# Two key tiles in a step for the last, 256-wide block of queries

## The chip, the cores and the metric

The kernel runs on one core of a Trainium2 chip, as one program in one launch. What counts is device time in microseconds (us) from start to end of the program. The core has a matrix engine (PE in the profile, with PEld for the loads of its stationary operand), a vector engine (DVE), an activation engine (ACT), a general engine (POOL) and an engine that issues DMAs (SP). PE writes only to PSUM, which has eight banks of 512 f32 in each of 128 partitions. DVE and ACT read PSUM; POOL works on SBUF.

## The reference

Two layers follow each other, each with a residual and a layer norm. The first is an attention over 3327 nodes by cosine, masked with a sparse adjacency matrix; the change does not touch it. The second is this:

```python
q = (x @ Wq.T).reshape(d, n, h)      # d = 128 groups, n = 3327 nodes, h = 8
k = (x @ Wk.T).reshape(d, n, h)
v = (x @ Wv.T).reshape(d, n, h)
a = jnp.einsum('dnh,dmh->dnm', q, k) * d ** (-0.5)
a = a + adj + adj
a = jax.nn.softmax(a, axis=2)
out = jnp.einsum('dnm,dmh->dnh', a, v)
out = out.reshape(n, h * d) @ Wo.T
```

So there are 128 independent attentions over 3327 x 3327 pairs, with an inner size of only 8, and each pair gets twice its adjacency added ahead of the softmax.

## The kernel before

Nodes are padded to 26 tiles of 128 (T = 26). Queries are cut into nine blocks (NB): eight of three tiles, 384 queries, and a last one of two tiles, 256 queries. The 128 attentions are taken four at a time, so there are 32 groups, and a *unit* is one block with one group: 288 units, the last 32 of them 256 wide. A unit runs 26 *steps*, one for each key tile, so the main loop (line 884) has 7488 steps, 832 of them in the last block. The four attentions of a group are called heads here; each has its own 32 rows of PE, since queries and keys stand in SBUF with 32 partitions for a head (line 228): a high and a low part of each number, times 8, times 2.

Scores stand in PSUM with keys on partitions and queries along the bank. The order of instructions on PE, ACT, DVE and POOL is the order of the code (a manual schedule), each engine taking its own in turn; the order on SP is the framework's. In one step:

- `shifts` (L805) puts minus the maximum of each query's scores into the two banks of `eb`, for two heads; `scores` (L811) adds query times key. ACT takes the exponential of both banks in one instruction (L921, tile `pb`), and POOL multiplies with `eT`, the exponential of twice the adjacency (L922).
- For the other two heads the same happens in two single banks `ea`, but the adjacency is added on PE: `add_adj` (L792) multiplies `aT` with twice the identity, in four column strips a head. ACT takes the exponential of each bank (L946, tile `pa`).
- `weigh` (L822) multiplies the weights `pa` and `pb` with the values and sums over the keys into one bank, `acc`, in four column strips, one a head. It handles the tile of two steps before (LAG = 2). Its operands are f32, and each product is two matmul records. After a unit's last tile, `take` (L833) copies `acc` out.
- `search` finds the maxima of a unit ahead of it: 33 steps ahead (T + AHEAD) it makes products of queries with keys in the other direction (`max_product`, L265), 512 keys at a time, and DVE reduces each to a maximum a query. In the 384-wide blocks a step has one *pair* (two heads, two banks, one reduce of 1024, L280) and one *single* (one head, one bank, a reduce of 512, L301). For the 256-wide units a step has two singles, of heads (2, 3) and (0, 1) in turn (line 237); these take banks from a pool of three (`at_n`, line 901), used in rotation.
- When a unit's maxima are there, `shift_parts` splits them into three bf16 parts, and late in the unit before, `shift_turn` (L778) transposes them on PE; ACT copies them to `cx` (L940).

PSUM is full: two banks `ea`, two `eb`, one `acc`, three for the search. In a step of the last block the search products use the rows of the same two heads as `eb` (line 904).

Of the kernel before, what the change touches and what calls it, by code (L numbers as in the profile page):

```python
# [10 lines left out]
F32 = mybir.dt.float32  # L11
# [8 lines left out]
P = 128  # L20
N = 3327
T = 26
# [23 lines left out]
def gnn_two_layers(  # L46
# [130 lines left out]
    def width(b):  # L177
        return min(QT, T - b * QT) * P
# [49 lines left out]
    def rows(a):  # L228
        return slice(32 * a, 32 * a + KR)
# [82 lines left out]
    def search(step):  # L312
        if step is not None:
            (max_pair if len(step[1]) == 2 else max_single)(*step)
# [403 lines left out]
    with ExitStack() as at:  # L718
# [15 lines left out]
        for vt in vts:  # L734
            nc.gpsimd.memset(vt[:, :, T - 1, :], 0.0)

        def load_adj_tile(b, j):
            n = width(b) // P
            nc.sync.dma_start(  # L739
                aT[:, j, : n * P].rearrange("p (q k) -> p q k", k=P),  # L740
                aT_s[b * QT : b * QT + n, :, j * P : (j + 1) * P].rearrange("q p k -> p q k"),
            )

        def exp_adj_tile(b, j):
            w = width(b)
            nc.scalar.activation(eT[:, j, :w], aT[:, j, :w], AF.Exp, scale=2.0)

        def load_values(u):

            u.vt = vts[u.i % 3]  # L750
            for first, n, rows in ((0, 112, T), (112, P - 113, T), (P - 1, 1, N - (P - 1) * T)):
                nc.sync.dma_start(
                    u.vt.rearrange("p g t r -> p g (t r)")[first : first + n, :, : rows * R9],
                    bass.AP(
                        tensor=v_s.tensor,
                        offset=v_s.offset + (4 * u.g * N + first * T) * R9,
                        ap=[[T * R9, n], [N * R9, 4], [1, rows * R9]],
                    ),
                )
            u.cx = sm.tile([P, QB], BF16, name="cx")  # L760

        def order_keys(u, j):

# [11 lines left out]
        def shift_turn(u, q, dst, start):  # L775
            for h in range(4):
# [8 lines left out]
                    skip_group_check=True,  # L785
                )

        def add_adj(e, u, j):

            for c in range(4):  # L790
                r = slice(32 * c, 32 * c + 32)
                nc.tensor.matmul(  # L792
                    e[r, : u.nq],
                    two[:, r],
                    aT[:, j, : u.nq],
                    start=False,
                    stop=True,
                    tile_position=(0, 32 * c),
                    skip_group_check=True,
                )  # L800

        def shifts(u, es, hs):
            for e, a in zip(es, hs):
                r = slice(32 * a, 32 * a + 3)
                nc.tensor.matmul(  # L805
                    e[:, : u.nq], one[r], u.cx[r, : u.nq], start=True, stop=False, skip_group_check=True
                )

        def scores(u, j, es, hs, stop):
            for e, a in zip(es, hs):  # L810
                nc.tensor.matmul(  # L811
                    e[:, : u.nq],
                    u.kx[rows(a), j * P : (j + 1) * P],
                    u.qx[rows(a), : u.nq],
                    start=False,
                    stop=stop,
                    skip_group_check=True,
                )

        def weigh(u, j, pts):  # L820
            for h in range(4):
                nc.tensor.matmul(  # L822
                    acc[32 * h : 32 * h + H + 1, : u.nq],
                    u.vt[:, h, j],
                    pts[h][:, : u.nq],
                    start=(j == 0),
                    stop=(j == T - 1),
                    tile_position=(0, 32 * h),
                )

        def take(u):
            ot = sm.tile([P, QB], F32, name="ot")
# [12 lines left out]
        with tc.manual_schedule(  # L845
# [31 lines left out]
            e = ps_b.tile([P, 2, 512], F32, name="eb")  # L877
            for q in range(QT):
                shift_turn(us[0], q, e[:, 0, q * P : (q + 1) * P], True)
            nc.scalar.copy(us[0].cx, e[:, 0, :QB])  # L880

            todo = []
            turn = []
            for s in range(NU * T + LAG):
                i, j = divmod(s, T)
                u = us.get(i)
                if u is not None:
                    if j == 2 and i + 2 < NU:
                        load_keys(new_unit(i + 2))
                        load_queries(us[i + 2], own.tile([P, QB], F32R, name="qx"))  # L890
                        load_values(us[i + 2])
                    if j == 12 and i + 4 < G4:
                        gather(i + 4)
                    k = s + T + AHEAD
                    pair, single = max_step(k) or (None, None)

                    behind = pair is not None and len(pair[1]) == 1
                    if behind and Banks.pair is not None:
                        Banks.pair = None
                        search_banks.close()  # L900
                        ps_n = at.enter_context(tc.tile_pool(name="at_n", bufs=3, space=PSUM))
                        Banks.single = lambda: ps_n.tile([P, 512], F32, name="m3")
                    if behind:
                        hs_b = pair[1] + single[1]
                    else:
                        hs_b = (2, 3) if pair is None else tuple(
                            h for h in range(4) if h not in pair[1]
                        )
                    hs_a = tuple(h for h in range(4) if h not in hs_b)

                    e_b = ps_b.tile([P, 2, 512], F32, name="eb")
                    b01 = [e_b[:, x] for x in range(2)]
                    shifts(u, b01, hs_b)
                    if not behind:
                        search(pair)
                    scores(u, j, b01, hs_b, True)
                    if behind:
                        search(pair)
                        search(single)
                    pt_b = pp.tile([P, 2, QB], F32, name="pb")  # L920
                    nc.scalar.activation(pt_b[:, :, : u.nq], e_b[:, :, : u.nq], AF.Exp)  # L921
                    nc.gpsimd.tensor_tensor(  # L922
                        pt_b[:, :, : u.nq],
                        pt_b[:, :, : u.nq],
                        eT[:, j, : u.nq].unsqueeze(1).to_broadcast([P, 2, u.nq]),
                        ALU.mult,
                    )
                    e_a = new_a()
                    shifts(u, e_a, hs_a)
                    if not behind:  # L930
                        search(single)
                    scores(u, j, e_a, hs_a, False)
                    free = e_a[0][:, QB:]
                    x = us.get(i + 1)
                    copies = []
                    q = j - (T - 4)
                    if x is not None and 0 <= q < x.nt:
                        shift_turn(x, q, free, False)
                        copies.append(
                            lambda: nc.scalar.copy(x.cx[:, q * P : (q + 1) * P], free)  # L940
                        )
                    pt_a = pp.tile([P, 2, QB], F32, name="pa")
                    for h, e in enumerate(e_a):
                        add_adj(e, u, j)
                    for h, e in enumerate(e_a):
                        nc.scalar.activation(pt_a[:, h, : u.nq], e[:, : u.nq], AF.Exp)  # L946
                    for f in copies:
                        f()
                    if x is not None and not x.b:
                        order_keys(x, j)  # L950
                        if j == T - 1:
                            keep_keys(x)
                    pts = {}
                    for x in range(2):
                        pts[hs_a[x]], pts[hs_b[x]] = pt_a[:, x], pt_b[:, x]
                    todo.append((u, j, pts))

                    if k % (2 * T) in (T, 2 * T - 1):
                        v = us.get(k // (2 * T) * 2 + (k % (2 * T) > T))
                        if v is not None:  # L960
                            shift_parts(v)
                if s >= LAG:
                    w = todo.pop(0)
                    weigh(*w)
                    if w[1] == T - 1:
                        take(us.pop(w[0].i))

                if turn and turn[0][0] <= s:
                    exp_adj_tile(*turn.pop(0)[1:])
                if u is not None and i + 1 < NU and units[i + 1][0] != u.b:  # L970
                    load_adj_tile(u.b + 1, j)
                    turn.append((s + 5, u.b + 1, j))
# [96 lines left out]
```

## Time and profile before

| what | value |
|---|---|
| median of 3 runs | 15258.02 us (15257.38 to 15259.73) |
| profiled execution, own time | 15255.29 us |
| its span, first to last instruction | 15253.5 us |
| granted PE clock, mean | 0.996 |
| blocks 2 to 8, pb exponentials from 2438 to 13947 us | 1.98 us a step |
| last block, pb exponentials from 13947 to 15153 us | 1.45 us a step |
| PE, DVE, ACT, POOL busy over the span | 99%, 91%, 84%, 90% |

One profiled execution is a list of instructions with start and duration. A timeline line reads: start in us from the span's start, duration in us, engine, line of the kernel, operation, names of what is written and read, shapes, and how many equal instructions in a row are merged; in square brackets, if the engine sat idle before it, for how long and what ended that. The page's first part gives the busy time of each engine, its share of the span and its instructions. A windows line gives, for a stretch, its length, then busy time and number of instructions of each engine, the granted clock, the share of DMA engines in use and GB/s. A matmul's end in the trace is modelled, and matmuls overlap, so a busy PE is not PE at its peak.

### The profile page before, as it was taken

What the parts mean: (1) busy time and instruction counts of PE and PEld (TensorE: products, weight loads), DVE (VectorE), ACT (ScalarE), POOL (GpSimd) and SP (SyncE); (2) the same over time, 40 slices, a digit from 0 to 9 for tenths busy, and PEclk for the clock granted to TensorE, in tenths of its full rate; (3) what the DMA queues carried; (4) which work ended last, traced back from release to release, by engine and by line L of the source; (5) the groups of instructions that cost most, each with busy time, mean ns of one, the idle gap of its engine ahead of it and who ended that gap; (6) DMA issues with size and microseconds to landing.
All of it is one profiled execution on the core that took longest, in us unless ns stands there. A gap on an engine that the chain in (4) does not pass through costs nothing.

```text
span 15253.5 us, 495125 instructions
## 1 busy us (share of the span) xinstructions
PE 15089.0 (99%) x210460; PEld 6723.2 (44%) x210460; DVE 13878.6 (91%) x16267; ACT 12766.2 (84%) x25413; POOL 13770.0 (90%) x8926
## 2 busy tenths in 40 slices
PE   7899999999999999999999999999999999999999
PEld 5534444444444444444444444444444444444556
DVE  8889999999999999999999999999999999998886
ACT  7699998888888888888888888888888888888887
POOL 3489999999999999999999999999999999999888
PEclk9999999999999999999999999999999999999999
DMA  5632221111111111111111111111111111112212
GB/s 198 207 102 102 99 96 60 47 53 47 59 48 48 52 53 54 47 51 49 54 53 47 53 54 50 50 47 60 47 51 49 47 59 47 53 47 63 64 64 84
DMA packets 549346, 996.69 MB, mean 65 GB/s; under 512 B 148249, under 2 KB 492822, under 8 KB 500790
## 3 DMA queue, kind: packets, MB, share of 16 engines
q1 hardware_dynamic: 547126, 965.00, 19.5%
q8 instruction: 1648, 27.00, 0.8%
q14 instruction: 572, 4.69, 0.1%
HBM read 826.75 MB, written 192.54 MB: 67 GB/s over the span
## 4 chain that ended last, share of the span: by engine, by line
PE 95%; DVE 0%; ACT 0%; DMA 0%; SPq 0%; issue 0%; POOL 0%; ACTq 0%; DVEq 0%; POOLq 0%
PE acc L822 30%; PE ea L792 22%; PE m L265 17%; PE eb L805 13%; PE ea L805 9%; PE ea L811 2%; PE ea L778 1%; PE eb L811 1%; PE pp L1017 0%; PE pq L544 0%; PE sc L265 0%; DVE mx L280 0%; SPq L739 0%; DMA orow<-o_s 0%; ACT oT L1014 0%
## 5 line engine op out<-in xcount | busy, mean ns | idle before, releaser
L922 POOL TENSOR_TENSOR pb<-pb,eT 128x768 f32<-128x768 f32 (+1 forms) x7488 | 13176.7, 1767 | 906.8 <-ACT pb L921 466.4
L280 DVE TENSOR_REDUCE mx<-m 128x2 f32<-128x1024 f32 x6369 | 7807.8, 1226 | 959.1 <-PE eb L811 507.6
L921 ACT ACTIVATE pb<-eb 128x768 f32<-128x768 f32 (+1 forms) x7488 | 5903.9, 788 | 2163.9 <-PE eb L811 1810.5
L265 PE MATMUL m<-kn,qx 32*128 32x512 f32 (+1 forms) x23128 | 6553.6, 463 | 0.0
L946 ACT ACTIVATE pa<-ea 128x384 f32<-128x384 f32 (+1 forms) x14976 | 6336.5, 477 | 27.1 <-PE ea L792 10.4
L822 PE MATMUL acc<-pb,vt 128*9 128x384 f32 (+1 forms) x29952 | 5903.1, 474 | 0.1
L822 PE MATMUL acc<-pa,vt 128*9 128x384 f32 (+1 forms) x29952 | 5903.1, 474 | 0.0
L301 DVE TENSOR_REDUCE mx<-m 128x1 f32<-128x512 f32 x7139 | 4798.0, 681 | 134.4 <-PE m L265 49.5
L805 PEld LDWEIGHTS <-one 3*128 3x128 bf16 x29952 | 1412.1, 91 | 5554.0 <-issue 4659.7
L792 PE MATMUL ea<-aT,two 128*32 128x384 bf16 (+1 forms) x59904 | 3714.3, 325 | 0.0
L811 PE MATMUL eb<-qx,kn 32*128 32x384 f32 (+1 forms) x13312 | 3027.0, 451 | 0.0
L811 PE MATMUL ea<-qx,kn 32*128 32x384 f32 (+1 forms) x13312 | 2933.5, 432 | 0.0
L265 PEld LDWEIGHTS m<-kn,qx 32*128 32x128 f32 x23128 | 2723.0, 182 | 206.0 <-DVE mx L301 4.4
L805 PE MATMUL ea<-cx,one 3*128 3x384 bf16 (+1 forms) x14976 | 2802.3, 324 | 0.1
L805 PE MATMUL eb<-cx,one 3*128 3x384 bf16 (+1 forms) x14976 | 2464.3, 326 | 16.6 <-ACT cx L880 16.5
L822 PEld LDWEIGHTS acc<-pa,vt 128*9 128x9 f32 x29952 | 1415.7, 91 | 395.1
L822 PEld LDWEIGHTS acc<-pb,vt 128*9 128x9 f32 x29952 | 1415.8, 91 | 393.5 <-POOL pb L922 0.6
L792 PEld LDWEIGHTS <-two 128*32 128x32 bf16 x59904 | 936.8, 94 | 1388.9 <-issue 1155.0
L811 PEld LDWEIGHTS eb<-qx,kn 32*128 32x128 f32 x13312 | 1277.1, 189 | 0.0
L811 PEld LDWEIGHTS ea<-qx,kn 32*128 32x128 f32 x13312 | 1231.2, 182 | 36.7 <-issue 3.3
L305 DVE TENSOR_REDUCE mx<-m 128x2 f32<-128x512 f32 x1148 | 777.7, 682 | 10.7 <-PE m L265 2.6
L566 POOL CAST high<-row 128x512 fp32r<-128x512 f32 x104 | 104.4, 1004 | 366.0 <-ACT row L561 255.8
(130 smaller groups left out, 5881.7 us busy)
## 6 DMA issues: line engine op xcount, KB each, us to landing
kn<-kp_s SPq DMA_DIRECT2D x512, 832.0 KB
vt<-v_s SPq DMA_DIRECT2D x288, 409.5 KB
kn<-kq_s SPq DMA_DIRECT2D x64, 832.0 KB
qx<-qp_s SPq DMA_DIRECT2D x1016, 48.0 KB
kn<-in_adj_dram SPq DMA_DIRECT2D x25, 1663.5 KB
qp_s<-qn_s SPq DMA_DIRECT2D x64, 416.0 KB
kp_s<-kx SPq DMA_DIRECT2D x32, 832.0 KB
kq_s<-kn_s SPq DMA_DIRECT2D x64, 415.9 KB
```

What stands on the lines that cost most here:

```text
L265: nc.tensor.matmul(dst, u.qx[rows(a), q * P : (q + 1) * P], u.km[rows(a), k0:k1], start=True, stop=True,)
L280: nc.vector.tensor_reduce(u.mx[:, h, qs[0], c], m, axis=AX.X, op=ALU.max)
L301: nc.vector.tensor_reduce(u.mx[:, a, qs[0], c : c + 1], m, axis=AX.X, op=ALU.max)
L305: nc.vector.tensor_reduce(u.mx[:, a, qs[0] : qs[1] + 1, c], m.rearrange("p (q k) -> p q k", q=2), axis=AX.X, op=ALU.max,)
L778: nc.tensor.matmul(dst[r], parts[u.i % 2][:, q, h], unit, start=start, stop=True, tile_position=(0, 32 * h), skip_group_check=True,)
L792: nc.tensor.matmul(e[r, : u.nq], two[:, r], aT[:, j, : u.nq], start=False, stop=True, tile_position=(0, 32 * c), skip_group_check=True,)
L805: nc.tensor.matmul(e[:, : u.nq], one[r], u.cx[r, : u.nq], start=True, stop=False, skip_group_check=True)
L811: nc.tensor.matmul(e[:, : u.nq], u.kx[rows(a), j * P : (j + 1) * P], u.qx[rows(a), : u.nq], start=False, stop=stop, skip_group_check=True,)
L822: nc.tensor.matmul(acc[32 * h : 32 * h + H + 1, : u.nq], u.vt[:, h, j], pts[h][:, : u.nq], start=(j == 0), stop=(j == T - 1), tile_positio ...
L921: nc.scalar.activation(pt_b[:, :, : u.nq], e_b[:, :, : u.nq], AF.Exp)
L922: nc.gpsimd.tensor_tensor(pt_b[:, :, : u.nq], pt_b[:, :, : u.nq], eT[:, j, : u.nq].unsqueeze(1).to_broadcast([P, 2, u.nq]), ALU.mult,)
L946: nc.scalar.activation(pt_a[:, h, : u.nq], e[:, : u.nq], AF.Exp)
```

## The change

In the last block a step now handles two key tiles (`js` = 2). Each bank of `ea` and `eb` holds the 256 queries against tile j in its first half and against tile j + 1 in its second. Shifts, adjacency, exponentials and POOL's product become 512 a bank; `cx` holds the shifts twice, and `aT` and `eT` lie packed by the block's width, so that two tiles are 512 in a row. Scores and weighing are done for each of the two tiles, 256 wide, as before. The searches of two steps come together: four singles, of heads (0, 1) and then (2, 3), while `eb` belongs to heads (2, 3) and `ea` to (0, 1). The lag of the weighing stays two steps, which is now four tiles. The next shifts are turned in the free half of `acc`, since `ea` has none left. The tiles `pa` and `pb` become 512 wide a head for all blocks.

The order on PE in a new step is: shifts of eb, first search, scores of eb (4), second search, shifts of ea, scores of ea (4), third and fourth search, adjacency (8), weighing (16 records).

```diff
+        def of_keys(a, b, j, n=1):
+
+            w = width(b)
+            return a.rearrange("p t q -> p (t q)")[:, j * w : (j + n) * w]
...
-            u.cx = sm.tile([P, QB], BF16, name="cx")
+            u.js = 1 if u.nt == QT else 2
+            u.n = u.js * u.nq
+            u.cx = sm.tile([P, 512], BF16, name="cx")
...
+        def keep_shift(u, q, n, src):
+
+            c = u.cx[:, : u.n].rearrange("p (x k) -> p x k", x=u.js)[:, :, q * P : (q + n) * P]
+            nc.scalar.copy(c, src.unsqueeze(1).to_broadcast([P, u.js, n * P]))
...
-                    e[r, : u.nq],
+                    e[r, : u.n],
                     two[:, r],
-                    aT[:, j, : u.nq],
+                    of_keys(aT, u.b, j, u.js),
...
+            for x in range(u.js):
+                for e, a in zip(es, hs):
+                    nc.tensor.matmul(
+                        e[:, x * u.nq : (x + 1) * u.nq],
+                        u.kx[rows(a), (j + x) * P : (j + x + 1) * P],
+                        u.qx[rows(a), : u.nq],
...
+            for x in range(u.js):
+                for h in range(4):
+                    nc.tensor.matmul(
+                        acc[32 * h : 32 * h + H + 1, : u.nq],
+                        u.vt[:, h, j + x],
+                        pts[h][:, x * u.nq : (x + 1) * u.nq],
...
+                if u is not None and j % u.js:
+                    continue
...
-                    k = s + T + AHEAD
-                    pair, single = max_step(k) or (None, None)
+                    ks = [s + T + AHEAD + x for x in range(u.js)]
+                    found = [max_step(k) or (None, None) for k in ks]
+                    pair, single = found[0]
+                    four = found if u.js == 2 and pair is not None else None
...
+                    if four is not None:
+                        hs_b = tuple(h for h in range(4) if (h,) not in (pair[1], single[1]))
...
                     shifts(u, b01, hs_b)
-                    if not behind:
+                    if four is not None:
+                        search(pair)
+                    elif not behind:
                         search(pair)
                     scores(u, j, b01, hs_b, True)
-                    if behind:
+                    if four is not None:
+                        search(single)
+                    elif behind:
                         search(pair)
                         search(single)
-                    pt_b = pp.tile([P, 2, QB], F32, name="pb")
+                    pt_b = pp.tile([P, 2, 512], F32, name="pb")
...
                     shifts(u, e_a, hs_a)
-                    if not behind:
+                    if not behind and four is None:
                         search(single)
                     scores(u, j, e_a, hs_a, False)
+                    if four is not None:
+                        for step in four[1]:
+                            search(step)
...
-                if s >= LAG:
+                if u is None or len(todo) > LAG:
                     w = todo.pop(0)
                     weigh(*w)
-                    if w[1] == T - 1:
+                    if w[1] == T - w[0].js:
                         take(us.pop(w[0].i))
+                if u is not None and u.js == 2 and j == T - 4:
+                    x = us.get(i + 1)
+                    if x is not None:
+                        for q in range(2):
+                            shift_turn(x, q, acc[:, 256 + q * P : 256 + (q + 1) * P], False)
+                        keep_shift(x, 0, 2, acc[:, 256:])
```

More of the change, by code (lines that the diff above doesn't have):

```diff
@@ L739, in load_adj_tile @@
             nc.sync.dma_start(
-                aT[:, j, : n * P].rearrange("p (q k) -> p q k", k=P),
+                of_keys(aT, b, j).rearrange("p (q k) -> p q k", k=P),
                 aT_s[b * QT : b * QT + n, :, j * P : (j + 1) * P].rearrange("q p k -> p q k"),
@@ L744, in exp_adj_tile @@
         def exp_adj_tile(b, j):
-            w = width(b)
-            nc.scalar.activation(eT[:, j, :w], aT[:, j, :w], AF.Exp, scale=2.0)
+            nc.scalar.activation(of_keys(eT, b, j), of_keys(aT, b, j), AF.Exp, scale=2.0)
         def load_values(u):
@@ L805, in shifts @@
                 nc.tensor.matmul(
-                    e[:, : u.nq], one[r], u.cx[r, : u.nq], start=True, stop=False, skip_group_check=True
+                    e[:, : u.n], one[r], u.cx[r, : u.n], start=True, stop=False, skip_group_check=True
                 )
         def scores(u, j, es, hs, stop):
[L810 to L818, printed above, removed]
-        def weigh(u, j, pts):
[L821 to L829, printed above, removed]
+            for x in range(u.js):
[4 more added lines that the diff above has]
+                        u.qx[rows(a), : u.nq],
+                        start=False,
+                        stop=stop,
+                        skip_group_check=True,
+                    )
+        def weigh(u, j, pts):
+            for x in range(u.js):
[4 more added lines that the diff above has]
+                        pts[h][:, x * u.nq : (x + 1) * u.nq],
+                        start=(j + x == 0),
+                        stop=(j + x == T - 1),
+                        tile_position=(0, 32 * h),
+                        skip_group_check=True,
+                    )
         def take(u):
@@ L879, in gnn_two_layers @@
                 shift_turn(us[0], q, e[:, 0, q * P : (q + 1) * P], True)
-            nc.scalar.copy(us[0].cx, e[:, 0, :QB])
+            nc.scalar.copy(us[0].cx[:, :QB], e[:, 0, :QB])
             todo = []
@@ L886, in gnn_two_layers @@
                 u = us.get(i)
+                if u is not None and j % u.js:
+                    continue
                 if u is not None:
-                    if j == 2 and i + 2 < NU:
+                    if j == 2 * u.js and i + 2 < NU:
                         load_keys(new_unit(i + 2))
@@ L913, in gnn_two_layers @@
                     shifts(u, b01, hs_b)
-                    if not behind:
+                    if four is not None:
+                        search(pair)
+                    elif not behind:
                         search(pair)
                     scores(u, j, b01, hs_b, True)
-                    if behind:
+                    if four is not None:
+                        search(single)
+                    elif behind:
                         search(pair)
                         search(single)
-                    pt_b = pp.tile([P, 2, QB], F32, name="pb")
-                    nc.scalar.activation(pt_b[:, :, : u.nq], e_b[:, :, : u.nq], AF.Exp)
+                    pt_b = pp.tile([P, 2, 512], F32, name="pb")
+                    nc.scalar.activation(pt_b[:, :, : u.n], e_b[:, :, : u.n], AF.Exp)
                     nc.gpsimd.tensor_tensor(
-                        pt_b[:, :, : u.nq],
-                        pt_b[:, :, : u.nq],
-                        eT[:, j, : u.nq].unsqueeze(1).to_broadcast([P, 2, u.nq]),
+                        pt_b[:, :, : u.n],
+                        pt_b[:, :, : u.n],
+                        of_keys(eT, u.b, j, u.js).unsqueeze(1).to_broadcast([P, 2, u.n]),
                         ALU.mult,
@@ L929, in gnn_two_layers @@
                     shifts(u, e_a, hs_a)
-                    if not behind:
+                    if not behind and four is None:
                         search(single)
                     scores(u, j, e_a, hs_a, False)
-                    free = e_a[0][:, QB:]
+                    if four is not None:
+                        for step in four[1]:
+                            search(step)
                     x = us.get(i + 1)
@@ L936, in gnn_two_layers @@
                     q = j - (T - 4)
-                    if x is not None and 0 <= q < x.nt:
+                    if u.js == 1 and x is not None and 0 <= q < x.nt:
+                        free = e_a[0][:, QB:]
                         shift_turn(x, q, free, False)
[L939 to L942, printed above, removed]
+                        copies.append(lambda: keep_shift(x, q, 1, free))
+                    pt_a = pp.tile([P, 2, 512], F32, name="pa")
                     for h, e in enumerate(e_a):
@@ L945, in gnn_two_layers @@
                     for h, e in enumerate(e_a):
-                        nc.scalar.activation(pt_a[:, h, : u.nq], e[:, : u.nq], AF.Exp)
+                        nc.scalar.activation(pt_a[:, h, : u.n], e[:, : u.n], AF.Exp)
                     for f in copies:
@@ L956, in gnn_two_layers @@
                     todo.append((u, j, pts))
[L958 to L961, printed above, removed]
-                if s >= LAG:
+                    for k in ks:
+                        if k % (2 * T) in (T, 2 * T - 1):
+                            v = us.get(k // (2 * T) * 2 + (k % (2 * T) > T))
+                            if v is not None:
+                                shift_parts(v)
+                if u is None or len(todo) > LAG:
                     w = todo.pop(0)
                     weigh(*w)
-                    if w[1] == T - 1:
+                    if w[1] == T - w[0].js:
                         take(us.pop(w[0].i))
-                if turn and turn[0][0] <= s:
+                if u is not None and u.js == 2 and j == T - 4:
[4 more added lines that the diff above has]
+                        keep_shift(x, 0, 2, acc[:, 256:])
+                while turn and turn[0][0] <= s:
                     exp_adj_tile(*turn.pop(0)[1:])
```

## The prediction

> **What bounds it now.** I read the page first, then the stages in windows, then one step of the last block in the timeline, then one step of the wider blocks, because the change gives a search a wait that only the wider blocks show.
>
> ```profile
> PE 15089.0 (99%) x210460; PEld 6723.2 (44%) x210460; DVE 13878.6 (91%) x16267; ACT 12766.2 (84%) x25413; POOL 13770.0 (90%) x8926
> ```
>
> Every engine is over 80% busy, so shares decide nothing. The windows give the size of what is touched:
>
> ```profile
> core 0: us, PE busy (x) PEld busy (x) DVE busy (x) ACT busy (x) POOL busy (x), PEclk, DMA share, GB/s
> 13947.00:15107.00 1160.00, 1159.91 (x21158) 670.91 (x21157) 1032.85 (x1630) 999.49 (x2496) 1038.76 (x921) 1.00 0.20 64
> 15107.00:15153.00 46.00, 46.00 (x780) 22.90 (x776) 0.00 (x0) 39.72 (x100) 41.22 (x37) 1.00 0.02 3
> ```
>
> The first row is the last block while the search still runs: 799 steps (799 pb products start in it). The second is its last 33 steps, whose searches were done 33 steps ahead (T + AHEAD). The clock is full in both. Together that is 1206 us, 8% of the span; nothing else should move. One step of the block:
>
> ```profile
> 14400.21 0.28 PE L805 MATMUL eb<-cx,one 3*128 3x256 bf16 x2
> ...
> 14400.28 0.26 PE L805 MATMUL ea<-cx,one 3*128 3x256 bf16 x1
> ...
> 14400.45 0.39 PE L265 MATMUL m<-kn,qx 32*128 32x512 f32 x2
> 14400.56 0.26 PE L805 MATMUL ea<-cx,one 3*128 3x256 bf16 x1
> ...
> 14400.87 0.40 PE L792 MATMUL ea<-aT,two 128*32 128x256 bf16 x8
> ...
> 14401.10 0.38 PE L822 MATMUL acc<-pb,vt 128*9 128x256 f32 x2
> ...
> 14401.28 0.66 ACT L946 ACTIVATE pa<-ea 128x256 f32<-128x256 f32 x2
> 14401.32 0.38 PE L822 MATMUL acc<-pb,vt 128*9 128x256 f32 x2
> ...
> 14401.64 0.28 PE L805 MATMUL eb<-cx,one 3*128 3x256 bf16 x2
> ...
> 14401.99 0.26 PE L805 MATMUL ea<-cx,one 3*128 3x256 bf16 x1
> ```
>
> The period is 1.43 (14400.21 to 14401.64). What closes it is a loop of ea banks: adjacency into ea (0.87), two pa exponentials (1.28 to 1.94), the second ea shift (1.99, 0.05 later, held for its bank), scores, next adjacency (2.30, again 1.43 on). In the 33 steps without any search a step also takes 1.43 (starts at 15130.75 and 15132.18), so the search does not bound this block. PE stands idle in front of 14400.56, and DVE and POOL have slack (two reduces of 0.68, one product of 1.28).
>
> A step of a 384-wide block shows what a search costs when its bank is not free:
>
> ```profile
> 8001.28 0.68 DVE L301 TENSOR_REDUCE mx<-m 128x1 f32<-128x512 f32 x1
> ...
> 8001.58 0.18 PEld L265 LDWEIGHTS m<-kn,qx 32*128 32x128 f32 x2
> ...
> 8002.02 0.18 PEld L265 LDWEIGHTS m<-kn,qx 32*128 32x128 f32 x1
> ...
> 8002.02 0.18 PEld L811 LDWEIGHTS ea<-qx,kn 32*128 32x128 f32 x2
> 8002.13 1.23 DVE L280 TENSOR_REDUCE mx<-m 128x2 f32<-128x1024 f32 x1 [0.17 <-PE eb L811]
> ...
> 8002.43 0.12 PEld L792 LDWEIGHTS <-two 128*32 128x32 bf16 x8 [0.23 <-issue]
> 8002.44 0.51 PE L792 MATMUL ea<-aT,two 128*32 128x384 bf16 x8
> ...
> 8002.77 0.49 PE L822 MATMUL acc<-pb,vt 128*9 128x384 f32 x2
> ```
>
> The step starts at 8001.58. Its first searches load weights at once, and their reduce starts at 8002.13, 0.55 after the start. The single search has one bank: its weight load starts at 8002.02, 0.06 after the reduce of the step before ended (8001.28 + 0.68), and the scores' weights, next in the program, load right behind it. So the wait holds the weight load, and PE's queue behind it. From that load to the adjacency's is 0.41.
>
> **The change, part by part.** Times are in us and count from a step's first shift, its start.
>
> *Merged exponentials and product.* pb takes 0.597 at 512 elements and 0.812 at 768, so about 1.03 at 1024; pa 0.38 and 0.49, so 0.60 at 512. ACT works 2.2 in a double step, where four pa and two pb took 2.5. POOL takes 1.276 at 512 and 1.829 at 768, so 2.38 (by the slope) to 2.55 (twice 1.276); I take 2.4. All three lie beside PE in what follows, at nothing; POOL decides only from a period below 2.4. The ea loop becomes adjacency to pa 0.5, first to second pa 0.5, second 0.6, shift 0.05, shift to adjacency 0.6: 2.25 for two key tiles instead of 2.86. That loop is gone as the bound.
>
> *PE's own order.* Half as many changes between the row-wise work (shifts, scores, searches) and the column-wise work (adjacency, weighing). The row-wise work is spread over all four row groups; unhindered, I put its end, and so the adjacency's load, near 0.87, as late as now. From adjacency to weighing: 0.23 at 256 (14400.87 to 14401.10), 0.33 at 384, so 0.44 at 512. From weighing to the next start: 0.54 now; two more passes of 0.215 (14401.10 to 14401.32) make 0.97. Adjacency to next start is thus 1.41. Unhindered PE needs 0.87 + 1.41 = 2.28.
>
> *Four searches on three banks: the added wait.* at_n has three banks, used in turn. Now two fills a step never meet a busy one. With four in a double step, the first three take banks whose readers belong to the step before; the fourth takes the bank that the first of the same step filled, and waits for that reduce. The chain: start to first reduce 0.55 (the pair's row; the new first search stands at the same place, behind the first shifts); the reduce 0.69 (L301 in this block: 678 to 694 ns, the long ones after idleness); 0.06 to the weight load; 0.41 to the adjacency's load. Sum 1.71 instead of 0.87. Queued behind the waiting load are the adjacency, the weighing and the next start, and behind the adjacency pa; DVE's next work, the second and third reduce, runs beside and is done before. The period is 1.71 + 1.41 = 3.12, against 2 x 1.43 = 2.86. Could DVE be late for the first reduce? Four reduces end near 3.06, before 3.12 + 0.55. Bounds: if the wait fell on the matmul alone, with weights loaded before, 0.11 less (the 0.18 weight load's part ahead of the stream), 3.01; if every reduce and hand-over took its longest row, 3.15. I take 3.12, since 8002.02 shows load and wait together.
>
> A rule can be weighed here. Row: the ea shift ran at 14400.28, before the searches (14400.45) that precede it in the program, so PE can pass a matmul held by the array; no row shows one passing a wait on a semaphore. The Trainium skill, *TensorE: Matmul & The Clock Gate* (Part 2), says matmuls stay in program order and only weight loads are pulled ahead. By the rule the fourth search holds everything, 3.12; if the passing of 14400.28 held here too, the sum would be that of the first rival.
>
> *Per unit.* Now 1160 - 799 x 1.43 = 17 us go to the turns of the next shifts, their copies, take and the narrow searches, over 30.7 units, mostly because they sit in ACT's loop. In the new step ACT has slack; the eight turn matmuls in acc cost about 0.16 on PE (230 ns each, four side by side, twice), the narrow searches some 0.15: 10 us.
>
> *The last 33 steps.* No search, so no wait: 16.5 double steps at POOL's 2.4 are 40 us instead of 46; the last product and weighing, twice as large, give back 1 to 2.
>
> *The 384-wide blocks.* pb rows become 512 apart, so the product is 2 x 384 instead of 768 in a row. The nearest strided row, 2 x 256 in 1.276, is at most 0.06 over two thirds of 1.829. POOL has 0.15 free in a step of 1.98 there, so nothing. Loads and DMAs per unit are the same, one step later at most, and the stage moves 64 GB/s at a DMA share of 0.20: nothing.
>
> *Sum.* 399.5 x (3.12 - 2.86) = +104; per unit -7; tail -5: **+92 us**. The profiled execution took 15255.3 (span 15253.5), 2.7 under the median 15258.0; on the median that gives **15350**, 0.6% slower. Its own range, from 3.01 (+48) to 3.15 with the per-unit 17 us kept (+111) and some margin, is 15300 to 15380.
>
> **Rivals.** *The fourth search holds nobody* (PE passes it, or its bank is free in time): then DVE is the bound at 4 x 0.63 = 2.53 (1032.85 us over 1630 instructions). 399.5 x (2.53 - 2.86) - 12 = -144: 15114. It speaks for it that PE and DVE both have room; against it, the scores waiting behind the search at 8002.02. It decides from an adjacency earlier than 1.45, where the period falls under 2.86. *It holds, but for 0.15 to 0.3 less than summed*, because the first reduce starts earlier than the pair's did or releases sooner: a period of 2.81 to 2.96, within 30 us of before, about 15260. No row is that short. *The 384-wide product gets slower than its slack*: every 10 ns over 0.15 us costs 6656 x 0.01 = 67 us; at 0.20 it would be 15350 + 333 = 15680. The 2 x 256 row speaks against it.
>
> **The numbers.** Forecast 0.76, first rival 0.13, second 0.08, third 0.03. A difference under 0.2% (30 us) cannot be told from none. Faster 0.13, same 0.08, slower 0.79. The range leaves out the first rival, the third and a margin: 15240 to 15400.
>
> **What would show it.** In a step of the last block, 3.12 from first eb shift to the next; the fourth L265 weight load 0.06 after the end of the step's first L301, near 1.30; the adjacency's load near 1.71 and pa's two of 0.60 behind it; idle PEld in front of L265 released by DVE mx L301, some 0.5 in each of 400 steps; pb of POOL 2.4 with idle time after. A fourth load before the first reduce's end, or a period under 2.86, proves the main step wrong; a 384-wide step other than 1.98 proves the other.

## The result and the profile after

The changed kernel took 15342.23 us (median of 4 runs, 15340.33 to 15343.92); the kernel before, run beside it, 15258.88. The ratio is 1.0054, 95% interval 1.0042 to 1.0066: slower by 0.5%, 83 us, where 92 had been forecast. The profiled execution took 15343.92 with a span of 15342.1, granted clock 0.996.

The windows of the last block, with the search and without, columns as before:

```profile
13952.00:15198.00 1246.00, 1127.26 (x16306) 590.09 (x16305) 994.97 (x1627) 871.18 (x1265) 968.66 (x520) 1.00 0.18 59
15198.00:15237.00 39.00, 39.00 (x608) 21.44 (x600) 1.69 (x4) 33.45 (x52) 38.03 (x21) 1.00 0.01 3
```

The first stretch had 1160 us, the second 46. Every engine is busy for less time than before, and PE, which had been busy all the time, now leaves 119 us idle. Busy time shrank and the time grew, so it is a wait. One double step in the timeline, cut, from its start (the first shifts' weight load) to the next:

```profile
14357.72 0.09 PEld L816 LDWEIGHTS <-one 3*128 3x128 bf16 x2 [0.43 <-issue]
...
14358.08 0.18 PEld L265 LDWEIGHTS m<-kn,qx 32*128 32x128 f32 x1
...
14358.27 2.48 DVE L301 TENSOR_REDUCE mx<-m 128x1 f32<-128x512 f32 x4 [0.63 <-PE m L265]
14358.42 0.28 PE L823 MATMUL ea<-qx,kn 32*128 32x256 f32 x2
...
14359.01 0.18 PEld L265 LDWEIGHTS m<-kn,qx 32*128 32x128 f32 x1 [0.51 <-DVE mx L301]
...
14359.43 0.12 PEld L803 LDWEIGHTS <-two 128*32 128x32 bf16 x8 [0.24 <-issue]
...
14359.88 0.38 PE L835 MATMUL acc<-pa,vt 128*9 128x256 f32 x2
...
14359.94 1.09 ACT L971 ACTIVATE pa<-ea 128x512 f32<-128x512 f32 x2 [0.47 <-PE ea L803]
...
14360.84 0.09 PEld L816 LDWEIGHTS <-one 3*128 3x128 bf16 x2 [0.43 <-issue]
```

The third search loads its weights at 14358.08, 0.36 after the start. The fourth (14359.01) waits 0.51 for DVE: the first of the four reduces began at 14358.27, and the fourth search's load begins 0.74 later, when that one reduce is over and while three are still to come. The ea scores had long been issued (14358.42), but the adjacency, next in the program, loads only at 14359.43. The view of waits over the first stretch puts a number on it:

```profile
engine line waited for: us in total, times, longest us
POOL pb L946 <- ACT pb L945: 270.6, 369, 1.1
DVE mx L301 <- PE m L265: 232.0, 369, 0.8
...
PEld m L265 <- DVE mx L301: 184.0, 369, 0.5
```

PE waits for DVE 0.5 in nearly every step (369 times in 400), and DVE waits for PE 0.6, as often. Neither is full; they wait for each other in turn. Before, PE did not stand idle ahead of a search's weight load in this block at all (the last number of this line, from the groups of 13947 to 15107):

```profile
L265 PEld LDWEIGHTS m<-kn,qx 32*128 32x128 f32 x1722 | 159.3, 187 | 0.0
```

### The profile page after: what moved, and what is told of

Same layout as the page of the kernel before. It is cut to its first block, busy times and chain, and to the rows that moved or that the text cites. A ratio compares the mean times of both kernels' runs of the same rounds, so it can differ in the third digit from the quotient of the medians.

```text
span 15342.1 us, 482633 instructions
## 1 busy us (share of the span) xinstructions
PE 15057.4 (98%) x205468; PEld 6637.0 (43%) x205468; DVE 13850.8 (90%) x16267; ACT 12647.7 (82%) x24134; POOL 13698.2 (89%) x8510
## 5 line engine op out<-in xcount | busy, mean ns | idle before, releaser
L945 ACT ACTIVATE pb<-eb 128x768 f32<-128x768 f32 (+1 forms) x7072 | 5829.3, 824 | 2191.1 <-PE eb L823 1888.9
L265 PE MATMUL m<-kn,qx 32*128 32x512 f32 (+1 forms) x23128 | 6781.1, 469 | 118.7 <-DVE mx L301 110.0
L971 ACT ACTIVATE pa<-ea 128x384 f32<-128x384 f32 (+1 forms) x14144 | 6250.5, 497 | 199.7 <-PE ea L803 188.9
L835 PE MATMUL acc<-pb,vt 128*9 128x384 f32 (+1 forms) x29952 | 5834.2, 474 | 1.0 <-POOL pb L946 1.0
L835 PE MATMUL acc<-pa,vt 128*9 128x384 f32 (+1 forms) x29952 | 5834.1, 474 | 0.0
L803 PE MATMUL ea<-aT,two 128*32 128x384 bf16 (+1 forms) x56576 | 3636.5, 334 | 0.0
L265 PEld LDWEIGHTS m<-kn,qx 32*128 32x128 f32 x23128 | 2799.2, 181 | 410.6 <-DVE mx L301 189.1
L816 PE MATMUL ea<-cx,one 3*128 3x384 bf16 (+1 forms) x14144 | 2544.6, 334 | 0.1
L816 PE MATMUL eb<-cx,one 3*128 3x384 bf16 (+1 forms) x14144 | 2391.9, 335 | 16.6 <-ACT cx L894 16.6
```

The lines of the kernel that those rows point to most:

```text
L265: nc.tensor.matmul(dst, u.qx[rows(a), q * P : (q + 1) * P], u.km[rows(a), k0:k1], start=True, stop=True,)
L803: nc.tensor.matmul(e[r, : u.n], two[:, r], of_keys(aT, u.b, j, u.js), start=False, stop=True, tile_position=(0, 32 * c), skip_group_check= ...
L816: nc.tensor.matmul(e[:, : u.n], one[r], u.cx[r, : u.n], start=True, stop=False, skip_group_check=True)
L835: nc.tensor.matmul(acc[32 * h : 32 * h + H + 1, : u.nq], u.vt[:, h, j + x], pts[h][:, x * u.nq : (x + 1) * u.nq], start=(j + x == 0), stop ...
L945: nc.scalar.activation(pt_b[:, :, : u.n], e_b[:, :, : u.n], AF.Exp)
L971: nc.scalar.activation(pt_a[:, h, : u.n], e[:, : u.n], AF.Exp)
```

## The experiments

All change only the order or the content of a double step of the last block; line numbers of their traces differ a little, and the edits are shown in part. Each ratio is to the kernel before, run beside it: 15259.56 us for the first four, 15263.23 for the last two.

**e1_no_fourth: without the fourth search.**

```diff
+            if u.b == NB - 1:
+                nc.gpsimd.memset(new_unit.mx, 0.0)
...
                     if four is not None:
-                        for step in four[1]:
-                            search(step)
+                        search(four[1][0])
```

> The changed kernel without the fourth search of each double step (its product and its reduce; a quarter of the maxima of the last block are left out, their tile is filled with zeros instead). My theory, that the fourth search's bank wait sets the step: the adjacency's first weight load comes at 0.91 after the step's start instead of 1.71, PE needs 2.32, and POOL's product becomes the bound at 2.37 (as in the last steps without search, 2.28 and 2.44 in turn). 399.5 x (3.12 - 2.37) = -300, so about 15045 us. Rival, that PE's longer matmuls and doubled weighing set the step and the wait only fills time that is idle anyway: 3.0 to 3.12, 15290 to 15342 us. Rival, that DVE's total work sets it: 3/4 of 3.12 = 2.34, about 15030 us, which this run does not tell from the first.

Measured: 15059.48 us, ratio 0.9868 (0.9855 to 0.9882), 14 above the expectation. From its timeline, the start, the adjacency's load and POOL back to back:

```profile
14299.76 4.73 POOL L948 TENSOR_TENSOR pb<-pb,eT 128x1024 f32<-128x1024 f32 x2
...
14300.90 0.09 PEld L818 LDWEIGHTS <-one 3*128 3x128 bf16 x2 [0.43 <-issue]
...
14301.88 0.12 PEld L805 LDWEIGHTS <-two 128*32 128x32 bf16 x8
```

The adjacency comes 0.98 after the start (0.93 in the median; 0.91 was expected), POOL runs without a gap (it idles 7 us of the stage's 963), and a step takes 2.39 in the median, 2.42 in the mean with the narrow searches. Without the fourth search the merged kernel is 200 us faster than the kernel before; with it, it is 83 slower. Not all of that is the wait, since e1 does less work; but a step got 0.73 shorter, while the fourth search itself holds PE only 0.42 (from its load at 14359.01 to the adjacency's at 14359.43). PE's own work is refused as the cause; DVE's total work is not, as had been said.

**e2_short_first: the first reduce reads half of its bank.**

```diff
-    def max_single(i, hs, qs, c):
+    def max_single(i, hs, qs, c, cols=512):
...
+                u.mx[:, a, qs[0], c : c + 1], m[:, :cols], axis=AX.X, op=ALU.max
...
                     if four is not None:
-                        search(pair)
+                        max_single(*pair, 256)
```

> The changed kernel, but the reduce of the first search of a double step reads 256 of its 512 columns (half of the keys are left out of a quarter of the maxima; the narrow searches stay). All matmuls stay. A reduce costs (1226 - 680) / 512 = 1.07 ns a column, so this one is 0.27 shorter. My theory, a chain through this very reduce: the fourth weight load and the adjacency come 0.27 earlier in 12 of 13 double steps, the step is 2.85 there, 399.5 x 0.27 x 12/13 = -100, so about 15242 us. Rival, PE's own work: no change, 15342 us. Rival, DVE's total work: the same 0.27 less, so only the third experiment tells that one apart.

Measured: 15243.8 us, ratio 0.9989 (0.9980 to 0.9999), 2 from the expectation. The groups of DVE in the middle of the block:

```profile
L301 DVE TENSOR_REDUCE mx<-m 128x1 f32<-128x512 f32 x962 | 604.0, 681 | 0.0
L301 DVE TENSOR_REDUCE mx<-m 128x1 f32<-128x256 f32 x320 | 135.9, 425 | 202.2 <-PE m L265 202.2
```

The short one takes 425 ns against about 690 for a first reduce after idleness, 0.265 less, and the median step fell from 3.118 to 2.852, 0.266 less. All matmuls were kept, so PE's own work is refused here too. Of the idle time ahead of the wide reduces, all stands ahead of this one (202 us) and none ahead of the other three (0.0): a step is as long as the way through this reduce.

**e3_fourth_later: the fourth search behind the adjacency.** All the work is kept.

```diff
-                        for step in four[1]:
-                            search(step)
+                        search(four[1][0])
...
                     for h, e in enumerate(e_a):
                         add_adj(e, u, j)
+                    if four is not None:
+                        search(four[1][1])
```

> The changed kernel with all its work; the fourth search stands behind the adjacency on PE, ahead of the weighing. My theory: its bank is free by then (weight load at about 1.46 against 1.30 for the bank), nothing waits for it; the adjacency's load comes at 0.91, and PE pays two more changes between row-wise and column-wise work: 0.91 + 0.55 (adjacency and drain) + 0.42 (search to the weighing's load) + 0.97 = 2.85. 399.5 x (2.85 - 3.12) = -108, about 15234 us, near the kernel before. Rival, DVE's total work sets the step: unchanged, 15342 us. Rival, the extra changes cost more than the wait: over 15342 us.

Measured: 15241.16 us, ratio 0.9987 (0.9978 to 0.9996), 7 above the expectation. PE in one step, which starts at 14299.53:

```profile
14300.44 0.61 PE L803 MATMUL ea<-aT,two 128*32 128x512 bf16 x8
14300.99 0.50 PE L265 MATMUL m<-kn,qx 32*128 32x512 f32 x1
14301.42 0.39 PE L835 MATMUL acc<-pa,vt 128*9 128x256 f32 x2
...
14302.40 0.39 PE L816 MATMUL eb<-cx,one 3*128 3x512 bf16 x2
```

Adjacency at 0.91, fourth search at 1.46, weighing at 1.89, next start at 2.87 (2.85 expected). The view of waits still lists weight loads of searches behind a reduce in e3 (156 us, 368 times), but from 14000 to 14900 no search's load starts within 0.18 of a reduce's end, where a load that waits for its bank comes 0.05 behind it; so the bank had been free. The same four reduces fit into 2.87, so DVE's total work, the rival that e1 and e2 had left, is refused: place, not amount.

**e4_weigh_between: the weighing between the two halves of the row-wise work.** All the work is kept. The order on PE is shifts and scores of eb with two searches, weighing, shifts and scores of ea, two searches, adjacency.

```diff
+                    if u.js == 2:
+                        weigh_next()
+                        if j == T - 4:
+                            turn_next(i)
                     e_a = new_a()
                     shifts(u, e_a, hs_a)
...
                 if u is None or len(todo) > LAG:
-                    w = todo.pop(0)
-                    weigh(*w)
...
+                    weigh_next()
```

> The changed kernel with all its work in another order on PE: shifts and scores of eb with the first two searches, then the weighing of the tiles from two steps before (and the turns), then shifts and scores of ea with the last two searches, then the adjacency. My theory: the fourth search comes at about 1.55 after the start, when its bank has been free since 1.30; PE needs 0.56 for the first part, 0.97 for the weighing, 0.56 for the second part, 0.55 for the adjacency, 2.63 in all; the second search may wait 0.03 for DVE. A step of 2.66: 399.5 x (2.66 - 3.12) = -184, and +4 in the last 16 steps, where PE instead of POOL becomes the bound: about 15162 us, 0.6% under the kernel before. Rival, DVE's total work: 15342 us. Rival, the ea loop of before returns, because the adjacency is now at the end of the step: pa ends 1.6 after it and the next ea shift stands 1.2 behind the next start, so not under 2.86 only if a step is shorter than 2.4; unlikely, 15260 us at worst.

Measured: 15238.95 us, ratio 0.9986 (0.9977 to 0.9995). A little faster than the kernel before, by 0.1%, but 77 above the expectation; the step takes 2.85, not 2.66. The timeline from the last two searches on:

```profile
14329.87 0.50 PE L265 MATMUL m<-kn,qx 32*128 32x512 f32 x2
14329.90 0.58 PE L823 MATMUL ea<-qx,kn 32*128 32x256 f32 x4
...
14330.56 1.29 DVE L301 TENSOR_REDUCE mx<-m 128x1 f32<-128x512 f32 x2 [0.38 <-PE ea L823]
...
14330.95 0.39 PE L816 MATMUL eb<-cx,one 3*128 3x512 bf16 x2
...
14331.30 0.18 PEld L265 LDWEIGHTS m<-kn,qx 32*128 32x128 f32 x1
```

The searches' matmuls end at 14330.37 (14329.87 + 0.50), but the reduce starts at 14330.56, and the trace says that the scores of ea released it: they end at 14330.48 and stand ahead of these searches in the program. So the third reduce is late, and the second search of the next step, which needs its bank, loads at 14331.30, 0.35 after that step's start; the weighing behind it is late as well. The wait for a bank had moved, not gone.

**e5_search_first: the last two searches ahead of ea's shifts and scores.** This is e4 with the two searches moved up, and with the old order in the steps without search; the edit is shown against e4.

```diff
-                    if u.js == 2:
+                    if four is not None:
                         weigh_next()
                         if j == T - 4:
                             turn_next(i)
+                        for step in four[1]:
+                            search(step)
                     e_a = new_a()
...
-                    if four is not None:
-                        for step in four[1]:
-                            search(step)
```

> The kernel of e4 (all work kept) with the last two searches of a double step ahead of the shifts and scores of ea, directly behind the weighing; in the steps without search the order of the changed kernel again. My theory after e4: its second search waited until 0.35 after the start, because the third search's reduce started 0.19 after that search's matmul had ended, 0.08 after the scores of ea ahead of it in the program had; PE tells of a finished matmul only when those before it in the program are finished. So here the third reduce starts 0.05 after its own matmul, 0.14 earlier; the second search loads weights at 0.19 instead of 0.35, the weighing comes at 0.61, and the step is 0.61 + 0.98 + 0.56 + 0.55 = 2.70. 400 x (3.12 - 2.70) = -168 against the changed kernel: about 15174 us, 0.56% under the kernel before. Rival, that DVE's four reduces with their hand-overs or the wait for the third reduce itself set e4's step, and not the order in which PE tells: 2.85 as in e4, less 4 for the last steps: 15235 us.

Measured: 15169.99 us, ratio 0.9939 (0.9927 to 0.9952), 4 from the expectation, and the fastest version that does all the work. The same place in its timeline:

```profile
14307.51 0.50 PE L265 MATMUL m<-kn,qx 32*128 32x512 f32 x2
...
14308.04 1.29 DVE L301 TENSOR_REDUCE mx<-m 128x1 f32<-128x512 f32 x2 [0.20 <-PE m L265]
...
14308.62 0.09 PEld L816 LDWEIGHTS <-one 3*128 3x128 bf16 x2 [0.42 <-issue]
...
14308.79 0.18 PEld L265 LDWEIGHTS m<-kn,qx 32*128 32x128 f32 x1
```

The reduce starts 0.03 after its matmuls' end (14308.01), released by the search itself, the second search loads 0.17 after the start, and the median step is 2.69. Only the order of instructions on one engine differs from e4 in these steps. PE is busy all through this stage. A little waiting is left: the second search still loads only 0.05 after that reduce, which ends at 14308.73.

**e6_last_two_early: the same move in the changed kernel.** The lines that search `four[1]` stand ahead of `e_a = new_a()`; nothing else.

> The changed kernel with the last two searches of a double step ahead of the shifts and scores of ea, nothing else. If PE's queue holds everything behind a weight load that waits on a semaphore, the ea shifts start behind the fourth search's load at 1.29, the ea scores end 0.62 later at 1.91, the adjacency loads at 1.84 instead of 1.71 and the step is 3.25: 400 x 0.13 = +52, about 15394 us. Rival, that shifts and scores of ea pass the waiting search, as the ea shift passed the searches at 14400.28 in the kernel before: the fourth search alone sets the adjacency, 3.12 or a little less, about 15342 us.

Measured: 15398.81 us, ratio 1.0089 (1.0074 to 1.0105), 5 from the expectation. Its timeline at the waiting search:

```profile
14379.95 0.18 PEld L265 LDWEIGHTS m<-kn,qx 32*128 32x128 f32 x1 [0.75 <-DVE mx L301]
...
14379.95 0.09 PEld L816 LDWEIGHTS <-one 3*128 3x128 bf16 x2
...
14380.51 0.12 PEld L803 LDWEIGHTS <-two 128*32 128x32 bf16 x8
```

The shifts of ea use other rows and other banks than the search, and their banks were free; still they load in the same hundredth in which the search's wait ends. The median step is 3.25. Here a load that waits on a semaphore holds all of PE's program behind it. Against the kernel before beside it, the same move makes the changed kernel 52 us slower (135.6 instead of 83.4 over it), where from e4 to e5 it brought 73 (20.6 to 93.2 under it), some 4 of them in the last steps.

## Why the prediction was right

**The chain.** Forecast from the start: first reduce 0.55, fourth load 1.30, adjacency 1.71, next start 3.12. In the step above: 0.55, 1.29, 1.71, 3.12. The parts taken over from narrower rows held too: adjacency to weighing 0.45 (0.44 by extending 0.23 and 0.33), weighing to next start 0.96 (0.97). That the wait runs through the first reduce was shown by e2; that it is the place of the fourth search and not the work of DVE, by e3.

**Who is held.** The two readings weighed against each other, that PE passes a held search or that it does not, are settled by e6 for a load that waits on a semaphore: nothing passes, and the step grows to 3.25. The program order that the Trainium skill states (*TensorE: Matmul & The Clock Gate*, Part 2) holds there. It did not hold at 14400.28 before, where the ea shift started ahead of two searches (14400.45) whose banks were free.

**Merged work at nothing.** POOL takes 2.37 (2.4 was taken), pb 1.02, pa 0.60; POOL waits 271 us and is not the bound. In e1 (2.39 a step) it is, as the forecast said it would be from a period below 2.4. The loop of ea banks is gone: pa now waits 186 us for the adjacency.

**The term that was mis-sized** is that of the units. From the first pb of the last block, 800 key tiles took 1160.6 before and 1248.7 after, +88 where +104 - 7 = +97 was summed. The step's part is right: 400 x 3.118 - 800 x 1.43 = +103. But 1248.7 - 400 x 3.118 leaves 1.5 for turns and narrow searches, where 10 had been kept: one step in a unit takes 3.23, and the turns, placed behind the weighing, cost nothing that the steps show. So this term is -15, not -7.

**The rest.** After those 800 tiles the last pb comes 35.4 us later instead of 44.8, -9 (with POOL's 2.36 a step, forecast 2.4 and -6), and from there to the end it is 105.4 instead of 100.8; in the experiments 103.3 to 104.7, so 2.5 to 5 come back, where 1 to 2 were said. The two differences cancel but for 1 or 2 us. The profiled executions are 88.6 apart, not 83: another 5.3 lies ahead of the last block, whose first pb comes at 13947.4 before and 13952.6 after; in the experiments this place moves between 13947.6 and 13952.8, so the difference is not put down to the change.

**The rivals.** The first, that the fourth search holds nobody, is refused by the 369 waits; the second, a shorter hold, by the period of 3.118. What a merged step with four searches and no wait would take, no run shows: e1's 2.39 is set by POOL, with only three reduces for DVE. DVE's 995 us over 400 steps are 2.49 a step, near the 2.53 that the first rival was given. PE's unhindered 2.28 was somewhat low: it had the adjacency at 0.87 behind four searches, and with only three ahead it loads at 0.91 (e3); this decided nothing here. The third is refused as well: the 384-wide blocks run at 1.977 a step in blocks 2 to 7, as before, and POOL's product there takes 1.828, where it took 1.829.

## What to carry to other kernels

When steps are merged, count the buffers against the fills of *one* merged step, not against the ratio of fills to steps: with more fills than banks, the last fill waits for a consumer within the same step, and its whole latency (fill, hand-over, reduce, hand-over, refill) enters the period although no engine is full. Then ask where in its engine's program the waiting instruction stands, since all that follows waits along; a producer that must wait belongs where other work fills that time, here the weighing between two pairs of searches, and a producer whose consumer is urgent belongs ahead of longer work. A merge can be worth keeping once its fills are spread: the same merge cost 0.5% in one order and gained 0.6% in another.

## What the runs showed that had not been expected

In these runs PE tells of finished matmuls in program order, although it starts them out of it. In e4 a search's result was 0.19 old when its reduce started, 0.08 after the end of the scores ahead of it in the program; in e5, with nothing unfinished ahead, the reduce started 0.03 after the end of its search. The times at which PE's semaphore rises, which the traces also hold, say the same. In e4 it rises at 14330.50, 14330.53 and 14330.57, once for the scores and once for each search, and not at 14330.37, when the searches had ended; in e5 it rises at 14308.02 and 14308.05, right behind them. Over some 330 reduces of each run, from 14000 to 14950, the first rise comes 0.12 after the searches' end in e4 and 0.01 in e5 (medians). A matmul's end is modelled in the trace, but in the same way in both runs. It was not tried with other forms of matmul.
